# A graph layer on one core: which points of TensorE's order hold the gathers around the products with src rows

## The chip, the cores and the metric

The kernel runs on one core of one Trainium2 chip. The metric is the device time of one execution in microseconds (us), taken as the median of several runs; less is better.

## The reference

There are 12,500 nodes with 32 features and 400,000 directed edges, sorted by their target node. The layer normalizes the nodes' rows, passes each edge through a small network, and takes per node the maximum over its incoming edges:

```python
h = jnp.maximum(_layernorm(x), 0.0)
e_feat = jnp.concatenate([h[src], h[dst], edge_attr_32], axis=-1)   # 400000 x 96
hid = jax.nn.relu(e_feat @ W1 + b1)                                 # 96 -> 64
v = hid @ W2 + b2                                                   # 64 -> 32
x_cand = jax.ops.segment_max(v, dst, num_segments=12500)
return x + jnp.maximum(x_cand, h[:, -32:])
```

## The kernel before, in words

The edges are cut into four stripes that lie side by side on the 128 partitions (32 features each), and each stripe into 196 chunks of 512 edges. The main loop takes two chunks a turn, an even one and an odd one, so it has 96 full turns. The first layer is a sum of three products into the same four banks of accumulators (`ph`): the edges' own rows (`ea`, `edges_into`), the target rows (`of` against a small window `qf` of rows, `windows_into`), and the source rows (`ht`, `rows_into`). All three go through `into_ph`, line 837, with 8 matmuls each a turn, which the profile shows as 16 records.

The source rows `h[src]` are the costly part, and they are fetched in two ways. Of the 16 columns of 128 edges that a chunk has, 12 (in some chunks 11) are gathered by GpSimd with an indirect DMA each (line 186, `gh`). The other 4 or 5 are made on TensorE by products with one-hot matrices (`tile(c, m)`, line 351, 14 matmuls each), of which VectorE then picks the wanted row (a multiplication `one`, line 358, and a maximum, line 359). VectorE also transposes all rows into `ht` (lines 375 and 378).

A turn's order on TensorE is written out by hand (the scheduling is manual for all engines): products `ea`, `of`, `ht`; the transposes of finished results `tr` (line 703); the one-hot tiles `a1`, `a2`, `a3` of the even chunk; the second layer `l2` (line 871); two products `lv` (line 727); the tiles `b0` to `b3` of the odd chunk; and `n0`, the first tile of the next even chunk. GpSimd meanwhile issues the gathers for a later turn: 12 of the even chunk (slots 0 to 11) and 12 of the odd one (slots 12 to 23). Their buffers would let them run ahead, so a table, `HELD` (line 72), spreads them: it ties a slot to a point of another engine's order, and the gather in that slot waits until that point has been passed. `hold` looks a slot up, and `passes` records the instruction that is the point:

```python
def passes(iteration, name, ins):
    passed[iteration, name] = ins
def hold(c, i, ins):
    at = HELD.get(i + c % 2 * (K - MM))
    if at and c // 2 - at[0] >= 0:
        waiting.append((ins, (c // 2 - at[0], at[1])))
...
passes(c // 2, "ea", into_ph(ph, [(w1c, loaded[c + x][0]) for x in range(2)], True, False))
...
passes(c // 2, "ht", into_ph(ph, [(w1a, ht[x]) for x in range(2)], False, True))
```

In the table `b1` is the last matmul of that tile on TensorE, `b1 max` the last step on VectorE for it, `ea`, `ht`, `tr`, `lv` and `n0` are points on TensorE, `relu` is one on ScalarE and `scan` one on VectorE. The number ahead of the name says how many turns ahead of the gather's own turn the point lies (`n0` is recorded under a number one lower than its place would give, so 3 with `n0` is the end of the same turn as 3 with `b3`; the `ea` and `ht` with a 2 come right behind it). A slot without an entry waits for none of these points; it goes when the gather before it on GpSimd has been issued, its buffer is free and the gather eight before it has landed.

Of the kernel before, what the change touches and what calls it, by code (L numbers as in the profile page):

```python
# [68 lines left out]
END = LATE - 16  # L69
PIECE = 2 * A0  # L70
GP = 3
HELD = {0: (3, 'b1'), 1: (3, 'b1 max'), 2: (3, 'b2'), 3: (3, 'b2 max'), 4: (3, 'b3'), 5: (3, 'b3 max'), 6: (3, 'n0'),
        8: (2, 'ea'), 9: (2, 'ht'), 10: (2, 'tr'), 12: (2, 'relu'), 13: (2, 'a1'), 14: (2, 'a1 max'), 15: (2, 'a2'),
        16: (2, 'a2 max'), 17: (2, 'a3'), 19: (2, 'lv'), 20: (2, 'scan'), 21: (2, 'b0'), 22: (2, 'b0 max')}
BANKS = 7
SOON = {(3, 0): 'a0', (3, 6): 'a2', (4, 0): 'a3', (4, 6): 'b0', (5, 0): 'b1', (5, 6): 'b2'}
# [14 lines left out]
def gnn_kernel(ctx, tc, x, src, src_mm, src_x, src_t, dst, dst_end, dst_ext, lo, lo_c, ends_b, edge_attr, weights, w1, w2, b2, out):  # L91
# [133 lines left out]
# [4 lines that stand above are left out]
# [1060 lines left out]
```

## Time and profile before

| | |
|---|---|
| three timed runs | 3557.04, 3555.01, 3553.36 us |
| median | 3555.01 us |
| profiled execution | 3587.46 us, of which the span is 3585.7 us |
| instructions in the span | 55,025 |
| TensorE busy (matmuls; weight loads, which overlap them) | 3293.3 us (92%); 2511.2 us (70%) |
| VectorE, GpSimd, ScalarE busy | 2437.4 us (68%), 2161.2 us (60%), 1402.3 us (39%) |
| gathers, line 186 | 2249 instructions, 2123.6 us, 944 ns each |

The profiled execution took 32 us (0.9%) more than the median, so times within the trace are read against its own 3587.46. A line of the timeline gives the start, the time, the engine, the line, the operation and what it writes and reads; in brackets stands the idle time of the engine ahead of it and what seems to have ended it. "issue" means that the profile names nothing.

### The profile page before, as it was taken

The numbers are of one execution on the slowest core, as the hardware profiler recorded it, in microseconds if no ns is written. First come the engines' busy times: TensorE is split into PE (matmuls) and PEld (weight loads), VectorE is DVE, ScalarE is ACT, GpSimd is POOL, SyncE is SP. The second block draws the span as 40 slices with busy tenths as digits, with TensorE's granted clock in tenths as the row PEclk, the third lists the DMA queues.
The fourth block names the chain that finished last, engine by engine and source line by source line (L and its number), as shares of the span: only waits on it lengthen the run. The fifth ranks groups of instructions, "written<-read, shape, count | busy, mean of one in ns | idle before, by whom it ended". The sixth has DMA issues, their size and how long they took to land.

```text
span 3585.7 us, 55025 instructions
## 1 busy us (share of the span) xinstructions
PE 3293.3 (92%) x18468; PEld 2511.2 (70%) x18468; DVE 2437.4 (68%) x4987; ACT 1402.3 (39%) x2276; POOL 2161.2 (60%) x2295
## 2 busy tenths in 40 slices
PE   5788999999999999999999999999999999999996
PEld 3466767776767677767776767777767777677773
DVE  6467667767677677676666666767666766666765
ACT  4233434343443333434333334333333344343342
POOL 6665666665666666656666666666666666666562
PEclk8799999999999999999999999999999999999997
DMA  5322222222222222222222222222222222221222
GB/s 188 82 60 58 58 59 58 71 50 58 68 63 52 58 65 63 52 58 62 62 56 64 62 59 56 59 63 66 50 63 63 62 53 62 61 66 50 59 58 64
DMA packets 183894, 227.88 MB, mean 64 GB/s; under 512 B 115365, under 2 KB 155445, under 8 KB 170806
## 3 DMA queue, kind: packets, MB, share of 16 engines
q10 hardware_dynamic: 36228, 109.11, 9.6%
q0 software_dynamic: 72992, 37.52, 7.7%
q1 hardware_dynamic: 74386, 77.71, 7.0%
q8 instruction: 145, 2.38, 0.3%
q14 instruction: 143, 1.17, 0.1%
HBM read 212.63 MB, written 11.47 MB: 63 GB/s over the span
## 4 chain that ended last, share of the span: by engine, by line
PE 70%; DVE 12%; issue 8%; another core or an unknown queue 4%; DMA 1%; ACT 1%; POOL 1%; SPq 1%; DVEq 0%; ACTq 0%; POOLq 0%
PE pv L351 53%; PE ph L837 12%; DVE one L358 3%; PE pv L871 3%; DVE hot L311 2%; DVE pv L878 2%; DVE ht L375 1%; PE pv L727 1%; POOL gh L186 1%; DVE sm L885 1%; PE pv L703 1%; DMA top_d<-wo 1%; DVE gm L359 1%; DVE m L892 0%
## 5 line engine op out<-in xcount | busy, mean ns | idle before, releaser
L186 POOL DMA_INDIRECT gh<-h_d,src_i x2249 | 2123.6, 944 | 1355.9 <-issue 511.8
L351 PE MATMUL pv<-hs,hot 128*128 128x448 f32 x10752 | 2369.3, 378 | 112.5 <-issue 76.7
L351 PEld LDWEIGHTS pv<-hs,hot 128*128 128x128 f32 x10752 | 2096.1, 197 | 326.8 <-issue 127.0
L358 DVE TENSOR_TENSOR one<-pv,mask 128x448 f32<-128x448 f32 x768 | 470.4, 612 | 982.7 <-issue 340.1
L862 ACT ACTIVATE hid<-ph,wt 128x512 f32<-128x512 f32 x392 | 244.2, 687 | 982.0 <-remote 491.2
L359 DVE TENSOR_REDUCE gm<-one 128x32 f32<-128x448 f32 x768 | 476.3, 620 | 26.4
L311 DVE TENSOR_TENSOR hot<-kb,consts 128x1024 fp32r<-128x1024 f16 (+1 forms) x379 | 445.4, 1194 | 0.0
L837 PE MATMUL ph<-ht,wt 32*64 32x512 f32 x1568 | 350.4, 696 | 95.0 <-issue 59.3
L325 ACT ACTIVATE hot<-away,ones 128x512 fp32r<-128x512 f32 x582 | 421.8, 725 | 36.9 <-remote 17.9
L324 ACT ACTIVATE away<-kb,key_n 128x512 f32<-128x512 f16 x582 | 415.7, 714 | 0.0
L718 ACT ACTIVATE wo<-pv 128x256 f32<-128x256 f32 x95 | 36.5, 384 | 689.7 <-remote 383.9
L837 PEld LDWEIGHTS ph<-ht,wt 32*64 32x64 f32 x1568 | 84.1, 141 | 294.3 <-issue 246.2
L878 DVE TENSOR_TENSOR_SCAN pv<-pb,kept,pv 128x512 f32<-128x512 bf16 x193 | 244.0, 1264 | 15.1 <-remote 15.0
L375 DVE STREAM_TRANSPOSE ht<-gh 128x96 f32<-128x96 f32 x774 | 207.9, 269 | 2.6
L697 ACT ACTIVATE sb<-m,wt 128x128 f32<-128x128 f32 x97 | 39.1, 403 | 423.1 <-DVE sm L885 239.4
L351 PE MATMUL pv<-hs,xg 128*128 128x448 f32 x760 | 169.2, 366 | 8.1 <-issue 8.1
L351 PEld LDWEIGHTS pv<-hs,xg 128*128 128x128 f32 x760 | 143.1, 189 | 21.4 <-issue 11.6
L837 PE MATMUL ph<-of,qf 32*64 32x512 f32 x1552 | 136.3, 606 | 14.3 <-ACT of L672 11.2
L672 ACT ACTIVATE of<-of,ones 128x512 f32<-128x512 f32 x194 | 140.6, 725 | 6.3
L892 DVE TENSOR_REDUCE m<-sm 128x64 f32<-128x512 f32 x194 | 133.1, 686 | 6.7
L671 ACT ACTIVATE of<-db,below 128x512 f32<-128x512 int32 x194 | 137.4, 708 | 0.0
L837 PE MATMUL ph<-ea,wt 32*64 32x512 f32 x1568 | 131.3, 619 | 3.7 <-issue 2.6
(139 smaller groups left out, 1309.4 us busy)
## 6 DMA issues: line engine op xcount, KB each, us to landing
ea<-in_edge_attr SPq DMA_DIRECT2D x49, 1024.0 KB
db<-in_dst_ext ACTq DMA_DIRECT2D x48, 1024.0 KB
gh<-h_d,src_i POOLq DMA_INDIRECT x2249
pb<-pen_d ACTq DMA_DIRECT2D x47, 512.5 KB
kb<-key_d ACTq DMA_DIRECT2D x47, 512.0 KB
top_d<-wo SPq DMA_DIRECT2D x752, 3.0 KB
qf<-q_d SPq DMA_DIRECT2D x392, 16.0 KB
q_d<-qs SPq DMA_DIRECT2D x6, 512.0 KB
```

The lines of the kernel that those rows point to most:

```text
L186: ins = nc.gpsimd.indirect_dma_start(out=parts[-1][:, i, :], out_offset=None, in_=h_d[:, :], in_offset=bass.IndirectOffsetOnAxis(ap=src_i[ ...
L311: nc.vector.tensor_tensor(hot_of(c)[:, start:stop], keys[c][:, None, :].to_broadcast([P, n, MM * P]), key_ps[:, start:stop, None].to_broad ...
L324: nc.scalar.activation(away, keys[c], AF.Square, bias=key_n[:, k:k + 1])
L325: nc.scalar.activation(hot_of(c)[:, k], away, AF.Relu, bias=ones, scale=-1.0)
L351: ins = nc.tensor.matmul(po, hot[k], hs[:, part, k].rearrange("p f a -> p (f a)"), start=(k == 0 and part == 0), stop=(k == A1 - 1 and par ...
L358: nc.vector.tensor_tensor(one, of_group, mask[:, None, :].to_broadcast([P, D, A0]), op=ALU.mult)
L359: passes(c // 2 - 1, "ab"[c % 2] + str(m) + " max", nc.vector.tensor_reduce(row, one, axis=AX.X, op=ALU.max))
L375: nc.vector.transpose(ht[:, r].rearrange("p k e -> p (k e)"), gh[c][part][:, :r.stop - r.start].rearrange("p k f -> p (k f)"))
L672: nc.scalar.activation(of, of, AF.Relu, bias=ones, scale=-1.0)
L837: ins = nc.tensor.matmul(ph[s][x * HID:(x + 1) * HID], w[g], e[g], start=start, stop=stop)
L862: passes(c // 2, "relu", nc.scalar.activation(hid[k], of, AF.Relu, bias=b1c))
L878: ins = nc.vector.tensor_tensor_scan(pv, pen[:, :C], pv, -LOW if before is None else before, op0=ALU.add, op1=ALU.max)
```

## The change

Only the table changes. Slot 6 loses its hold (`n0`). Slot 8 is held by the products with src rows (`ht`) where it was held by those with edge rows (`ea`). Slot 9 loses its hold (`ht`). Slot 7 had none and has none. Slot 10 still waits for `tr`.

```diff
-HELD = {0: (3, 'b1'), 1: (3, 'b1 max'), 2: (3, 'b2'), 3: (3, 'b2 max'), 4: (3, 'b3'), 5: (3, 'b3 max'), 6: (3, 'n0'),
-        8: (2, 'ea'), 9: (2, 'ht'), 10: (2, 'tr'), 12: (2, 'relu'), 13: (2, 'a1'), 14: (2, 'a1 max'), 15: (2, 'a2'),
+HELD = {0: (3, 'b1'), 1: (3, 'b1 max'), 2: (3, 'b2'), 3: (3, 'b2 max'), 4: (3, 'b3'), 5: (3, 'b3 max'),
+        8: (2, 'ht'), 10: (2, 'tr'), 12: (2, 'relu'), 13: (2, 'a1'), 14: (2, 'a1 max'), 15: (2, 'a2'),
         16: (2, 'a2 max'), 17: (2, 'a3'), 19: (2, 'lv'), 20: (2, 'scan'), 21: (2, 'b0'), 22: (2, 'b0 max')}
```

On GpSimd, in the middle of the program, these are the slots 4 to 11 of chunk 112, whose holds lie around the products with src rows of one turn of the main loop. `DMASW` is the landing of an earlier gather, `PE` and `DVE` are the points of TensorE's and VectorE's order:

```order
 L186 DMA gh<-h_d,src_i 128x32 [waits DMASW1_49,PE_49]
 L186 DMA gh<-h_d,src_i 128x32 [waits DMASW2_49,DVE_49]
-L186 DMA gh<-h_d,src_i 128x32 [waits DMASW3_49,PE_49]
-L186 DMA gh<-h_d,src_i 128x32 [waits DMASW4_49]
-L186 DMA gh<-h_d,src_i 128x32 [waits DMASW5_49,PE_49]
-L186 DMA gh<-h_d,src_i 128x32 [waits DMASW6_49,PE_49]
+L186 DMA gh<-h_d,src_i 128x32 [waits DMASW3_49]
+L186 DMA gh<-h_d,src_i 128x32 [waits DMASW4_49]
+L186 DMA gh<-h_d,src_i 128x32 [waits DMASW5_49,PE_49]
+L186 DMA gh<-h_d,src_i 128x32 [waits DMASW6_49]
 L186 DMA gh<-h_d,src_i 128x32 [waits DMASW7_49,PE_49]
 L186 DMA gh<-h_d,src_i 128x32 [waits DMASW0_49]
```

No gather has moved in the row; slots 6 and 9 have lost their wait for TensorE, and slot 8's wait, which reads alike, is now for a later matmul.

On TensorE, the products and the transpose of that same turn stand as they stood. These are the rows of before, and those of the changed kernel are the same:

```order
L837 MATMUL ph<-ea,wt 64x512 [waits PE_49]
L837 MATMUL ph<-ea,wt 64x512
L837 MATMUL ph<-ea,wt 64x512 [waits DVE_49]
L837 MATMUL ph<-ea,wt 64x512
L837 MATMUL ph<-of,qf 64x512 [waits DMAHW4_49,Activation_49]
L837 MATMUL ph<-of,qf 64x512 [waits Activation_49]
...
L837 MATMUL ph<-ht,wt 64x512 [waits DVE_49]
L837 MATMUL ph<-ht,wt 64x512 x6
L703 MATMUL pv<-ident,sb 128x128 [waits PE_49]
```

Slot 8 was tied to the last row with `ea` here and is now tied to the last with `ht`, the row ahead of the transpose; the order of the matmuls has not moved.

## The prediction

> **What bounds the kernel now.** I read the page first: the engines' busy time, the chain of work that ended last, then the groups of the lines that the change touches.
>
> ```profile
> PE 3293.3 (92%) x18468; PEld 2511.2 (70%) x18468; DVE 2437.4 (68%) x4987; ACT 1402.3 (39%) x2276; POOL 2161.2 (60%) x2295
> ...
> PE 70%; DVE 12%; issue 8%; another core or an unknown queue 4%; DMA 1%; ACT 1%; POOL 1%; SPq 1%; DVEq 0%; ACTq 0%; POOLq 0%
> PE pv L351 53%; PE ph L837 12%; DVE one L358 3%; PE pv L871 3%; DVE hot L311 2%; DVE pv L878 2%; DVE ht L375 1%; PE pv L727 1%; POOL gh L186 1%; DVE sm L885 1%; PE pv L703 1%; DMA top_d<-wo 1%; DVE gm L359 1%; DVE m L892 0%
> ...
> L837 PE MATMUL ph<-ht,wt 32*64 32x512 f32 x1568 | 350.4, 696 | 95.0 <-issue 59.3
> L837 PE MATMUL ph<-of,qf 32*64 32x512 f32 x1552 | 136.3, 606 | 14.3 <-ACT of L672 11.2
> L837 PE MATMUL ph<-ea,wt 32*64 32x512 f32 x1568 | 131.3, 619 | 3.7 <-issue 2.6
> ```
>
> TensorE sets the time, with 70% of the chain. The gathers that the change moves (GpSimd, L186) carry 1% of it. What is odd is the products of L837: the three kinds (edge rows, `of` against `qf`, src rows) have nearly the same count and shape, yet those with src rows (`ht`) cost 350.4 us and 95.0 of idle before them, the others 131.3 with 3.7 and 136.3 with 14.3.
>
> The waits show who makes whom wait there (total us, count, longest):
>
> ```profile
> PEld ph L837 <- issue: 353.7, 692, 2.7
> ...
> POOL gh L186 <- PE ph L837: 114.0, 83, 4.0
> ```
>
> TensorE's weight loads of L837 wait 353.7 us for "issue", that is for nothing the profile names; the gathers wait 114.0 us for L837, and those are the waits the change redistributes.
>
> In the timeline I took three turns of the main loop: A, where the products begin at 1997.57, B at 2034.31 and C at 1712.78. In A:
>
> ```profile
> 1999.71 0.94 POOL L186 DMA_INDIRECT gh<-h_d,src_i  x1 [0.30 <-issue]
> ...
> 2000.96 0.94 POOL L186 DMA_INDIRECT gh<-h_d,src_i  x1 [0.31 <-issue]
> ...
> 2001.97 3.48 PE L837 MATMUL ph<-ht,wt 32*64 32x512 f32 x10 [0.82 <-issue]
> ...
> 2003.41 0.36 PEld L837 LDWEIGHTS ph<-ht,wt 32*64 32x64 f32 x8 [1.30 <-issue]
> 2003.74 0.94 POOL L186 DMA_INDIRECT gh<-h_d,src_i  x1 [1.84 <-PE ph L837]
> ...
> 2005.38 0.47 PE L703 MATMUL pv<-ident,sb 128*128 128x128 f32 x1
> ...
> 2005.74 0.94 POOL L186 DMA_INDIRECT gh<-h_d,src_i  x1 [1.06 <-PE ph L837]
> ```
>
> The gathers shown are slots 6, 7, 8 and 9. Slot 6 goes 0.30 us behind the one before, the pitch of an unbroken stream: its hold (`n0`) had long been met. TensorE has gaps of 0.82 and 1.30 us without a named cause while the stream runs, and goes on at 2003.41, 1.5 us after slot 7's gather ends (2000.96 + 0.94). In B the hold of slot 6 bites:
>
> ```profile
> 2034.32 0.94 POOL L186 DMA_INDIRECT gh<-h_d,src_i  x1 [0.30 <-issue]
> ...
> 2036.85 0.94 POOL L186 DMA_INDIRECT gh<-h_d,src_i  x1 [1.58 <-PE ph L837]
> ...
> 2038.03 0.33 PE L703 MATMUL pv<-ident,sb 128*128 128x128 f32 x1
> ...
> 2038.10 0.94 POOL L186 DMA_INDIRECT gh<-h_d,src_i  x1 [0.30 <-issue]
> 2039.34 0.94 POOL L186 DMA_INDIRECT gh<-h_d,src_i  x1 [0.30 <-issue]
> ```
>
> Slot 6 waits 1.58 us, slots 7 and 8 follow unbroken, and the products are through by 2038.03. The windows give what each costs (us, TensorE busy, weight loads busy, granted clock, DMA share, GB/s): first the products of L837 in A, B, C, then each turn's stretch from the `lv` products to its end.
>
> ```profile
> 1997.57:2005.38 7.81, 6.68 (x48) 1.74 (x48) 0.81 0.18 27
> 2034.31:2038.03 3.72, 3.57 (x48) 1.03 (x48) 1.00 0.41 69
> 1712.78:1718.45 5.67, 5.07 (x48) 1.55 (x48) 1.00 0.09 12
> ```
>
> ```profile
> 2017.41:2034.30 16.89, 16.89 (x86) 15.58 (x84) 14.88 (x29) 7.48 (x12) 10.12 (x11) 1.00 0.16 25
> 2048.42:2069.65 21.23, 19.12 (x86) 16.88 (x84) 15.98 (x33) 7.47 (x12) 12.78 (x14) 0.92 0.22 64
> 1728.48:1746.45 17.97, 17.45 (x86) 15.43 (x84) 15.22 (x28) 7.47 (x12) 10.44 (x12) 1.00 0.13 21
> ```
>
> B saves in the products and pays behind them: 21.23 us for the same 86 products that take 16.89 in A and 17.97 in C. That is the core of my argument: the hindrance goes with the stream of gathers, and where a pause ends it early, another stretch meets it later.
>
> **The change, part by part.** No instruction is added or removed; the rows of TensorE, VectorE, ScalarE and SyncE stay in order. Four holds on GpSimd change, and with 96 turns each is priced by the turns in which it bites.
>
> *Slot 6 without a hold.* The gathers of slot 6 that waited over 0.61 us number 26, the first and the last being
>
> ```profile
> 207.14 0.94 POOL L186 DMA_INDIRECT gh<-h_d,src_i  x1 [1.68 <-remote]
> ...
> 3434.48 0.95 POOL L186 DMA_INDIRECT gh<-h_d,src_i  x1 [1.43 <-PE pv L1058]
> ```
>
> In the other 70 turns the hold is inert, as in A, and its removal does nothing. In the 26 GpSimd saves some 1.4 us, worth nothing by itself since it is off the chain. The indirect effect is that the stream then runs through slots 6 and 7 into the products, as in A and C: B becomes an A or a C. Whole turns are A 2034.30 − 1997.57 = 36.73, B 2069.65 − 2034.31 = 35.34, C 1746.45 − 1712.78 = 33.67 us. So B to A costs 1.39 us and B to C gains 1.67; in 26 turns that is +36 to −43 us. I take the middle, (1.39 − 1.67) / 2 × 26 = −4 us, since nothing says which of the two a freed turn becomes. What bears the middle out are sums over seven turns (columns: us; busy TensorE, weight loads, VectorE, ScalarE, GpSimd; clock; DMA; GB/s), which hold 1, 3, 2 and 3 turns in which slot 6 waited:
>
> ```profile
> 1573.26:1824.81 251.55, 238.07 (x1345) 182.13 (x1338) 173.60 (x358) 99.46 (x161) 152.87 (x163) 0.95 0.24 60
> 1824.81:2075.45 250.64, 237.62 (x1344) 182.95 (x1337) 174.38 (x359) 98.95 (x161) 153.51 (x163) 0.94 0.24 62
> 2326.50:2575.86 249.36, 237.10 (x1345) 183.11 (x1339) 173.53 (x358) 98.96 (x161) 152.90 (x163) 0.95 0.24 60
> 3076.75:3329.31 252.56, 238.74 (x1344) 181.69 (x1338) 174.59 (x363) 99.21 (x161) 153.82 (x164) 0.95 0.24 60
> ```
>
> They lie between 249.36 and 252.56 with no trend: both ends have seven turns with two or three such waits.
>
> *Slot 8 behind `ht` instead of `ea`, slot 9 without a hold.* Where slot 8 waited for `ea` (A, C), it now waits until slot 9's old time, 2005.74 in A, and slot 9 goes one pitch later (0.94 + 0.30 = 1.24 us). In A that is 2.00 us for slot 8 and 1.24 for slot 9. Behind them slots 10 to 14 are also one pitch later. The stream has a pause that takes it up: slot 15 waits 1.65 us for `a2`.
>
> ```profile
> 2014.58 0.94 POOL L186 DMA_INDIRECT gh<-h_d,src_i  x1 [1.65 <-PE pv L351]
> ```
>
> 1.65 − 1.24 leaves 0.41, so slot 15 goes when it went. Price 0; if that cover is gone, GpSimd, busy for 60% of the span, is 1.24 us late until the next pause. Rows gathered now are used a turn later, and a lag of a pitch reaches TensorE only if VectorE's transposes wait for them, which 1% of POOL in the chain bounds. What queues behind the waiting slot 8 is GpSimd's stream alone: slots 9 and 10, then the rest. SP and ACT issue no DMA behind it.
>
> *The stretch of products freed of slot 8's issue.* In A slot 8 starts at 2003.74, 1.64 us ahead of the transpose (L703, 2005.38); in C likewise:
>
> ```profile
> 1717.71 0.95 POOL L186 DMA_INDIRECT gh<-h_d,src_i  x1 [1.99 <-PE ph L837]
> ...
> 1718.45 0.33 PE L703 MATMUL pv<-ident,sb 128*128 128x128 f32 x1
> 1719.45 0.94 POOL L186 DMA_INDIRECT gh<-h_d,src_i  x1 [0.79 <-PE pv L703]
> ```
>
> There it is 0.74 us at full clock, and A's clock is 0.81 over the products, which alone could make up the difference. TensorE has already recovered when slot 8 goes, in both. So I give this 0, with a gain of up to 0.74 us in the some 50 turns of the 70 whose slot 8 waits so (in the rest VectorE is late and slot 5 waits instead), −37 us, as the lower end, and as the upper end +0: a gather fewer beside the products has no way to lengthen them.
>
> **The sum.** −4 + 0 + 0 = −4 us. The profiled execution has a span of 3585.7 us and took 3587.46; the median of the three timed runs, 3555.01, is 32 us less, so the trace shows a somewhat more hindered run than the usual. Carried over to the median: 3555 − 4, about 3551 us. Less than 0.2% (7 us) either way can't be told from no change in this kernel; the forecast is no change.
>
> [...] The row first: over the products the clock was 0.81 in A and 1.00 in B and C, and A is the turn with the longest gaps. [...]
>
> **The rivals.** *Faster.* The product stretch is now clear of gathers from slot 7 to its end in every turn, and what hindered B later (21.23) goes as well: freed turns become Cs (33.67), and half of the 0.74 us of slot 8 comes too. For: C exists with slot 6 unheld. Against: the whole-turn sums don't fall where slot 6 waits less. Time: 26 × 1.67 × 0.5 = 22, or with 50 × 0.37 = 18 about 40; I put it at 3555 − 30 = 3525 us, from −10 to −50.
>
> *Slower.* Slots 8 to 14 one pitch later close the pause of 1.65 us at slot 15, where it is shorter than 1.24, and the stream then runs unbroken into the second layer and the `b` tiles, as in B: 21.23 − 16.89 = 4.34 us in each such turn. It decides from two turns up (8.7 us). For: B's stream ran so, and paid. Against: A's pause is longer than the lag. If 1 in 10 of the 70 other turns loses its pause: 7 × 4.34 = +30, 3585 us. Freed turns that become As give the same sign: 26 × 1.39 = +36, 3591 us.
>
> *It doesn't do what it says.* With slot 6 inert in 70 turns, and `ht`'s signal arriving with `ea`'s in the others (B: slot 8 unbroken), the order on the chip hardly differs: 3555 us. It shares the forecast's case.
>
> **How the numbers follow.** No change, inert or balanced: 0.37. Faster, gathers out of the products: 0.36, more than slower because both its parts have a row and the lower end lies further from 0 with the products' term. Slower, the pause lost or As for Bs: 0.27. Range: the faster case down to −35 us (3520, a tenth left out below), the slower up to +28 us (3583, a tenth above). For the likeliest case alone: 3548 to 3562.
>
> **What would show it.** In the trace of after: slot 6 at a gap of 0.30 in nearly all turns; slot 8 behind the `ht` products and slot 9 at 0.30 behind slot 8; L837 `ht` near 350 us or up to 26 × 2 = 50 us more, given back from `lv` to the turn's end; seven turns still 249 to 253 us. Wrong would be: `ht` far below 350 us (the slot-8 term was mis-sized), or seven-turn sums that leave that band either way, slot 15 without a pause being the sign of the slower case.

## The result and the profile after

The changed kernel took 3662.35 us (median of 4 runs, 3653.06 to 3665.07) against 3554.19 us before: a ratio of 1.0303, 95% interval 1.0279 to 1.0327, or 108 us slower. That is outside the predicted range. On four other Trainium2 chips, which the later experiments met, before takes 2938 us, and on the one of them where the changed kernel ran, so does it; this is told below, and it is the larger surprise.

The page of the changed kernel shows where to look: the engines' busy times, the chain of work that ended last, and the groups of L186 and of the products with src rows.

```profile
PE 3371.0 (92%) x18468; PEld 2546.1 (70%) x18468; DVE 2433.4 (67%) x4987; ACT 1399.3 (38%) x2276; POOL 2161.2 (59%) x2295
...
PE 76%; DVE 11%; issue 8%; another core or an unknown queue 2%; DMA 1%; POOL 1%; ACT 0%; DVEq 0%; SPq 0%; ACTq 0%; POOLq 0%
...
L186 POOL DMA_INDIRECT gh<-h_d,src_i x2249 | 2124.1, 944 | 1424.3 <-issue 545.5
...
L837 PE MATMUL ph<-ht,wt 32*64 32x512 f32 x1568 | 390.8, 752 | 112.8 <-issue 67.0
```

GpSimd issues the same gathers at the same 944 ns and still carries 1% of the chain. The products with src rows rose from 350.4 to 390.8 us. The waits of the changed kernel (total, times, longest, us):

```profile
PEld ph L837 <- issue: 439.0, 782, 10.7
POOL gh L186 <- PE ph L837: 214.2, 55, 6.7
```

TensorE's nameless waits in L837 went from 353.7 to 439.0 us, as more turns are hindered. The gathers' waits for L837 went from 114.0 to 214.2 us, which is the new hold of slot 8. In the timeline, the turn that was B in the prediction now reads:

```profile
2069.24 0.94 POOL L186 DMA_INDIRECT gh<-h_d,src_i  x1 [0.30 <-issue]
...
2070.49 0.94 POOL L186 DMA_INDIRECT gh<-h_d,src_i  x1 [0.30 <-issue]
...
2071.73 0.94 POOL L186 DMA_INDIRECT gh<-h_d,src_i  x1 [0.30 <-issue]
...
2072.76 0.22 PEld L837 LDWEIGHTS ph<-ht,wt 32*64 32x64 f32 x3 [1.28 <-issue]
...
2072.98 0.94 POOL L186 DMA_INDIRECT gh<-h_d,src_i  x1 [0.30 <-issue]
2074.19 0.13 PEld L837 LDWEIGHTS ph<-ht,wt 32*64 32x64 f32 x1 [1.21 <-issue]
...
2075.59 0.23 PEld L837 LDWEIGHTS ph<-ht,wt 32*64 32x64 f32 x7 [1.27 <-issue]
...
2076.90 0.48 PE L703 MATMUL pv<-ident,sb 128*128 128x128 f32 x1
...
2077.24 0.94 POOL L186 DMA_INDIRECT gh<-h_d,src_i  x1 [3.32 <-PE ph L837]
```

The gathers are slots 4 to 8. Slots 6 (2071.73) and 7 (2072.98) follow unbroken where slot 6 had paused, the products' weights come in drops with 1.2 to 1.3 us between them, and slot 8 waits 3.32 us for the end of the products. The window over its products (us, TensorE, weight loads, clock, DMA share, GB/s) was 3.72 us in B and is now:

```profile
2069.23:2076.90 7.67, 5.92 (x48) 1.71 (x48) 0.96 0.46 82
```

To see whether this is paid back, I compared the same turns by number, from the first record of the `ea` products to the next turn's, for 86 turns (numbers 5 to 90). 24 of them had a pause at slot 6 before; 48 had neither that nor a late VectorE; in 14 VectorE was late. The numbers are means in us, worked out from the records of each trace. A half-clock window is here an unbroken stretch for which the trace gives TensorE's granted clock as half; these last 6.1 us on the mean before and 5.6 after.

| the same turns | before | changed | only slot 6 dropped | only slots 8, 9 changed |
|---|---|---|---|---|
| 24 that had paused: products | 4.59 | 8.16 | 7.92 | 6.63 |
| ... transpose to second layer | 8.86 | 9.94 | 9.92 | 9.60 |
| ... second layer to the end | 20.71 | 18.79 | 17.80 | 19.73 |
| ... whole turn | 34.16 | 36.90 | 35.64 | 35.95 |
| 48 others: whole turn | 36.55 | 36.50 | 35.87 | 36.47 |
| 14 with VectorE late | 36.48 | 36.45 | 35.91 | 36.49 |
| half-clock windows in the span | 72 | 97 | 83 | 86 |

Between these two traces the other turns stand as they stood. The 24 turns that had paused are 2.74 us longer each, 66 us, and the spans differ by 3651.3 − 3585.7 = 65.6. So the loss between the two traces lies in those turns whole: 3.57 us more in the products, 1.08 in the tiles behind them, 1.92 back later. The timed difference is 42 us larger than that of the spans, because the first profile of before was 32 us above its median and that of the changed kernel 9 below its own. No trace shows where these 42 us lie. The column "only slot 6 dropped" gives a hint: there the 48 other turns are 0.68 us shorter each than before's (35.87 against 36.55), 33 us in all. If before's slow profile lost its 32 us in such turns, then a usual run of before loses something there to the change as well, and the 66 us are only the part of the 108 that the traces locate.

### The profile page after: what moved, and what is told of

Its sections match the earlier page's. It is cut to its first block, busy times and chain, and to the rows that moved or that the text cites. A ratio compares the mean times of both kernels' runs of the same rounds, so it can differ in the third digit from the quotient of the medians.

```text
span 3651.3 us, 54835 instructions
## 1 busy us (share of the span) xinstructions
PE 3371.0 (92%) x18468; PEld 2546.1 (70%) x18468; DVE 2433.4 (67%) x4987; ACT 1399.3 (38%) x2276; POOL 2161.2 (59%) x2295
## 4 chain that ended last, share of the span: by engine, by line
PE 76%; DVE 11%; issue 8%; another core or an unknown queue 2%; DMA 1%; POOL 1%; ACT 0%; DVEq 0%; SPq 0%; ACTq 0%; POOLq 0%
PE pv L351 56%; PE ph L837 15%; PE pv L871 3%; DVE one L358 2%; DVE pv L878 2%; DVE hot L311 1%; PE pv L727 1%; PE pv L703 1%; DVE ht L375 1%; DVE sm L885 1%; DMA q_d<-qs 1%; DVE m L892 1%; POOL gh L186 1%; DVE gm L359 0%
## 5 line engine op out<-in xcount | busy, mean ns | idle before, releaser
L186 POOL DMA_INDIRECT gh<-h_d,src_i x2249 | 2124.1, 944 | 1424.3 <-issue 545.5
L351 PE MATMUL pv<-hs,hot 128*128 128x448 f32 x10752 | 2383.8, 380 | 80.0 <-issue 46.9
L351 PEld LDWEIGHTS pv<-hs,hot 128*128 128x128 f32 x10752 | 2120.3, 199 | 281.3 <-issue 80.0
L837 PE MATMUL ph<-ht,wt 32*64 32x512 f32 x1568 | 390.8, 752 | 112.8 <-issue 67.0
L837 PEld LDWEIGHTS ph<-ht,wt 32*64 32x64 f32 x1568 | 93.0, 150 | 333.6 <-issue 281.3
L837 PE MATMUL ph<-of,qf 32*64 32x512 f32 x1552 | 159.2, 638 | 21.7 <-issue 19.3
L351 PE MATMUL pv<-hs,xg 128*128 128x448 f32 x760 | 165.9, 363 | 1.4 <-issue 1.3
L351 PEld LDWEIGHTS pv<-hs,xg 128*128 128x128 f32 x760 | 142.6, 188 | 12.7 <-issue 3.0
L837 PE MATMUL ph<-ea,wt 32*64 32x512 f32 x1568 | 134.4, 626 | 9.4 <-issue 9.3
```

Source lines behind the costliest of these rows:

```text
L186: ins = nc.gpsimd.indirect_dma_start(out=parts[-1][:, i, :], out_offset=None, in_=h_d[:, :], in_offset=bass.IndirectOffsetOnAxis(ap=src_i[ ...
L351: ins = nc.tensor.matmul(po, hot[k], hs[:, part, k].rearrange("p f a -> p (f a)"), start=(k == 0 and part == 0), stop=(k == A1 - 1 and par ...
L837: ins = nc.tensor.matmul(ph[s][x * HID:(x + 1) * HID], w[g], e[g], start=start, stop=stop)
```

## The experiments

The diffs are against the kernel before, in the table `HELD`, unless the text names another. The first four ran on a chip where before takes 3555.22 us, as it did for the prediction; I call it the first chip.

**Only slot 6.**

```diff
-5: (3, 'b3 max'), 6: (3, 'n0'),
+5: (3, 'b3 max'),
```

> Only the hold of slot 6 is dropped; slots 8 (ea) and 9 (ht) stay held as before. Theory 'pause': the loss came from the 24 or so turns in which slot 6 waited and its pause let the products with src rows through (1.73 us there, 3.55 in the like turns after the change) and spared the turn a half-clock window; then this kernel has no pause at slot 6, some 97 half-clock windows against 72 before, and 3630 to 3665 us. Theory 'lag': the loss came from slots 8 to 14 going a pitch later; then this kernel stays within 15 us of before, 3540 to 3570 us.

Measured: 3576.05 us, ratio 1.0056 (1.0039 to 1.0072). Between the two theories: slower, but by 21 us. The profiled span, 3578.2 us, is 7 us below that of before's slow profile, so the traced numbers below compare turns and don't add up to the 21. The windows over the products and from `lv` to the end of the turn that was B:

```profile
2024.17:2031.64 7.47, 6.20 (x48) 1.75 (x48) 0.83 0.37 80
```

```profile
2043.63:2060.53 16.90, 16.90 (x87) 15.58 (x85) 14.95 (x32) 7.48 (x12) 10.18 (x11) 1.00 0.24 52
```

The products are as hindered as in the changed kernel (7.67), but the stretch behind falls from B's 21.23 to 16.90, the unhindered length. Here the gain is mostly given back, as I had forecast for the whole change: in the 24 turns 3.33 us more, 2.91 us less behind, and 1.06 in between at half clock.

**Only slots 8 and 9.**

```diff
-8: (2, 'ea'), 9: (2, 'ht'),
+8: (2, 'ht'),
```

> Slot 6 keeps its hold (n0); slot 8 waits for ht, slot 9 for nothing. Theory 'pause': about 24 turns keep the pause at slot 6, half-clock windows stay near 72, 3540 to 3575 us. Theory 'lag': the whole loss is here, 3630 to 3665 us. If both have a part, the excesses of this kernel and of the one that drops slot 6 alone add up to about 108 us.

Measured: 3617.22 us, ratio 1.0168 (1.0148 to 1.0187). Theory "lag" asked for 3630 us or more and isn't met. Theory "pause" alone, as I had put it, fails as well: 62 us come from the holds that I priced at nothing. But the trace shows that they act through the same pause. In the 24 turns slot 5 now starts 1.01 us behind the products' start, where it was 0.23 ahead. So `n0` has been met by the time slot 6 is reached, and 12 of the 24 pauses are gone; those turns take 2.49 us more, the 12 that kept it 1.09 more, and 46 of the 48 others 0.01. That is 12 x 2.49 + 12 x 1.09 = 43 us, and this profile's span, 3629.1, is 43 us above that of before. The lag that I had thought taken up at slot 15 reaches slot 5 of the next round: in the turn ahead of each of the 24, slots 9 to 12 go 0.79 us later than before on the mean, and slot 22 still 0.76. The rest of slot 5's 1.24 us is mostly that turn itself, which is 0.43 us shorter.

The two parts make 21 + 62 = 83 of the 108 us. Together they cost more: without the hold of slot 6 the late slots 8 and 9 lengthen the stretch behind the second layer in the 24 turns from 17.80 to 18.79, and the other 48 turns from 35.87 to 36.50.

**A pause at slot 6 in every turn.**

```diff
-6: (3, 'n0'), 8: (2, 'ea'), 9: (2, 'ht'),
+6: (2, 'ea'), 8: (2, 'ht'),
```

> The changed kernel with slot 6 held by the products with edge rows (ea) of the turn, a point right behind n0. Theory 'pause': the pause then comes in most turns, not in 24 only; products from their start to the transpose fall from 7.4 us to 4.6 to 6, half-clock windows from 97 to under 60, and the time to 3480 to 3560 us, part of it paid back behind the products (20.7 against 18.6 us there). Theory 'lag': slots 8 to 14 are as late as in the changed kernel, so 3640 us or more.

Measured: 3552.87 us, ratio 0.9998 (0.9986 to 1.0009). One hold at slot 6, put 16 records later in TensorE's order, takes back the whole 108 us of the changed kernel. (The number expected for theory "lag" isn't a test here, since the gathers are no longer late: slot 12 goes 11.45 us behind the start of the products on the mean, against 13.01 in the changed kernel and 11.73 before.) Slot 6 waits in all 72 turns without a late VectorE, products take 4.48 us on the mean (7.40 in the changed kernel, over the same 86 turns), and there are 55 half-clock windows (97). But the stretch from the second layer on takes 22.24 us (19.09), so that nothing is gained over before. Windows of two turns that follow each other, the products and the stretch from `b0` (us, TensorE, weight loads, VectorE, ScalarE, GpSimd, clock, DMA, GB/s):

```profile
2013.07:2018.12 5.05, 4.84 (x50) 1.48 (x50) 4.95 (x10) 0.07 (x1) 2.81 (x4) 1.00 0.47 76
2028.39:2052.04 23.65, 20.85 (x86) 17.23 (x84) 17.94 (x40) 7.46 (x12) 12.99 (x14) 0.86 0.20 58
```

```profile
2052.04:2055.18 3.14, 3.14 (x50) 1.09 (x50) 3.04 (x8) 0.00 (x0) 1.89 (x2) 1.00 0.24 36
2065.45:2085.41 19.96, 18.05 (x86) 15.42 (x84) 14.77 (x27) 7.48 (x12) 12.58 (x14) 1.00 0.11 16
```

The same 86 products take 23.65 us in the one and 19.96 in the other, against 16.90 unhindered, and the long one is at clock 0.86: this time the half-clock windows fall there.

**No gather beside the products.**

```diff
-6: (3, 'n0'), 8: (2, 'ea'), 9: (2, 'ht'),
+6: (2, 'ht'),
```

> Slots 6 to 9 all wait behind the products with src rows (6 is held by ht, 7 to 9 by nothing): no gather is issued beside them once slot 5 is out. Theory 'pause': products fall to 4 to 5 us in nearly all turns, half-clock windows under 40, 3450 to 3540 us, unless the stream, 2.5 us later at slot 12, loses its other pauses, which would bring it back to about 3560. Theory 'lag': slots 10 to 14 are 2.5 us later than in the changed kernel, and the time is above 3665 us.

Measured: 3656.97 us, ratio 1.0278 (1.0249 to 1.0308). My theory's number fails: the products are nearly free (4.04 us) but the stretch from the second layer takes 23.82 us, and there are 102 half-clock windows. Theory "lag" doesn't explain it: slot 12 goes 11.98 us behind the start of the products, 0.25 us later than before and 1.0 us earlier than in the changed kernel, where I had expected 2.5 us later, and still the kernel loses 102 us. The timeline shows what a long unbroken stream does, here beside the tile `b0`:

```profile
2078.80 0.95 POOL L186 DMA_INDIRECT gh<-h_d,src_i  x1 [3.57 <-PE pv L703]
...
2088.48 1.17 PE L351 MATMUL pv<-hs,hot 128*128 128x448 f32 x5
...
2088.80 0.95 POOL L186 DMA_INDIRECT gh<-h_d,src_i  x1 [0.30 <-issue]
...
2090.10 0.46 PE L351 MATMUL pv<-hs,hot 128*128 128x448 f32 x1 [0.45 <-issue]
...
2090.80 0.47 PE L351 MATMUL pv<-hs,hot 128*128 128x448 f32 x1 [0.24 <-issue]
2091.30 0.95 POOL L186 DMA_INDIRECT gh<-h_d,src_i  x1 [0.31 <-issue]
2091.50 0.36 PE L351 MATMUL pv<-hs,hot 128*128 128x448 f32 x1 [0.23 <-issue]
...
2092.90 0.36 PE L351 MATMUL pv<-hs,hot 128*128 128x448 f32 x1 [1.04 <-issue]
...
2094.32 3.95 PE L351 MATMUL pv<-hs,hot 128*128 128x448 f32 x11 [0.34 <-issue]
```

The stream starts at 2078.80 and is unbroken. For its first eight gathers the tiles run at full pace; from the tenth (2090.05) matmuls start 0.70 us or twice that apart, and they are free again at 2094.32, 2.07 us after the last gather ends (2091.30 + 0.95). Over the whole trace, counting pauses of over 0.41 us between the starts of two matmuls of L351 less the 0.20 that is usual, and leaving out the first gather of a run and what lies behind its last: 4 us lost in 1471 us beside the second to seventh gather of a run, 7 of 87 beside the eighth and ninth, 155 of 214 from the tenth on. Behind the last gather of the runs of ten and more, until the next gather, another 170 of 246 us are lost. The place in the turn isn't the reason: beside the one tile `b0`, in the six traces of this chip together, 14 of 602 us are lost beside the second to seventh gather of a run, 43 of 263 beside the eighth and ninth, 137 of 192 from the tenth on (186 of these 192 us lie in this kernel). Beside the products it begins earlier: in turn A of the prediction the gaps stand beside the sixth and seventh gather of a run. So on this chip the price of a gather goes with the length of the run ahead of it, and this ties the holds together: a pause moved away from one place makes the run longer at the next.

**A break in the long run, and the other holds: on a second chip.** Four more kernels of this kind, the kernel before among them, met another chip. The first is the changed kernel with one more edit, shown against the changed kernel:

```diff
-13: (2, 'a1'), 14: (2, 'a1 max'), 15: (2, 'a2'), 16: (2, 'a2 max'),
+13: (2, 'a2 max'),
```

> The changed kernel with slot 13 held by the maximum of a2 (a2 max) in place of a1, and slots 14 to 16 held by nothing: slots 8 to 16, which go nearly unbroken in the changed kernel, get a pause of 0.6 to 1.9 us in their middle. Theory 'runs' (TensorE loses its time late in a long unbroken run of gathers, eight and more beside the one-hot tiles): the stretch from the second layer to the turn's end falls from 19.1 us to about 18.5, and the time to 3590 to 3635 us. Theory 'lag' (what costs is that GpSimd is later): slots 13 to 16 are another 1 us later, and the time is 3660 us or more.

The next is before with `6: (2, 'ea')` for `6: (3, 'n0')`:

> The kernel before with slot 6 held by ea in place of n0; slot 8 (ea) and slot 9 (ht) as before. It differs from the third experiment (six_ea, 3553 us) only in slots 8 and 9. If moving slot 8 behind ht costs about 60 us on its own, as in the second experiment, this kernel takes 3480 to 3500 us. Theory 'runs', by which that cost comes from products already hindered and from the run behind them (nine gathers there, eight here): within 30 us of 3553, on the faster side, 3525 to 3553 us.

Then the third experiment with `13: (2, 'a3')` and nothing for 14 to 17:

> The third experiment (slot 6 behind ea, slot 8 behind ht) with slot 13 held by a3 and slots 14 to 17 by nothing, so that the run from slot 8 to 16 is broken by a pause of about 2 us where the one-hot tiles of the even chunk end. Theory 'runs': the stretch from the second layer to the turn's end falls from 22.2 to 20 or 21 us, and the time to 3450 to 3530 us. Theory 'lag': slots 13 to 16 are 2 us later, 3570 us or more.

And the kernel before, unchanged:

> The kernel before, unchanged, for a second profile, since the first took 3587 us where the timed runs have 3555. All theories: about 3555 us. Theory 'pause': 60 to 70 half-clock windows (72 in the first profile) and 24 to 35 turns in which slot 6 waits (24 there).

Measured: 2938.29, 2937.75, 2941.02 and 2938.29 us, where before's timed runs there gave 2938.23; ratios of 1.0003, 1.0003, 1.0006 and 0.9998, all with 1 inside the interval. No theory had this: before itself is 617 us faster than on the first chip. Its page there:

```profile
PE 2858.3 (97%) x18468; PEld 2369.3 (81%) x18468; DVE 2437.4 (83%) x4987; ACT 1396.8 (48%) x2276; POOL 2162.3 (74%) x2295
...
PE 91%; DMA 4%; DVE 2%; ACT 1%; issue 1%; POOL 0%; SPq 0%; ACTq 0%; DVEq 0%; POOLq 0%
...
L186 POOL DMA_INDIRECT gh<-h_d,src_i x2249 | 2124.9, 945 | 710.7 <-issue 384.5
```

GpSimd and VectorE are busy as long as on the first chip (2162.3 and 2437.4 us), a gather takes 945 ns as there, and "issue" fell from 8% of the chain to 1%. A turn's products in the timeline:

```profile
1649.96 0.94 POOL L186 DMA_INDIRECT gh<-h_d,src_i  x1 [0.30 <-issue]
1650.29 0.23 PEld L837 LDWEIGHTS ph<-ea,wt 32*64 32x64 f32 x16 [0.30 <-issue]
...
1651.21 0.94 POOL L186 DMA_INDIRECT gh<-h_d,src_i  x1 [0.30 <-DVE one L358]
...
1652.06 0.18 PEld L837 LDWEIGHTS ph<-ht,wt 32*64 32x64 f32 x8 [0.25 <-issue]
1652.46 0.94 POOL L186 DMA_INDIRECT gh<-h_d,src_i  x1 [0.30 <-issue]
1653.05 0.33 PE L703 MATMUL pv<-ident,sb 128*128 128x128 f32 x1
```

The gathers go unbroken across the products, and these take 1653.05 − 1650.29 = 2.76 us. 1986 us of the tiles' time lie beside the tenth or a later gather of a run, and 0.3 us of it are lost. The stream hinders nothing on this chip. GpSimd goes nearly without a pause there: a turn takes 29.47 us on the mean, and its 23 or 24 gathers at 1.25 us take 28.8 to 30.0. So the holds hardly bite: in the 86 turns slot 6 waited over 0.61 us 9 times.

**The changed kernel again, with two others: on a third chip.**

> The changed kernel once more, since kernels that differ only in the holds all took 2938 us on a second chip, where before took 2938 as well and the sequencers' register moves, up to 0.72 us on the first chip, took 0.03 us. Theory 'hindered sequencers': the loss of 108 us needs that hindrance; where before takes 2938 us this kernel takes 2933 to 2944 us, and where before takes 3555 it takes 3645 to 3670. Rival: the later gathers cost something of their own, and this kernel is slower by 10 us or more on either chip.

> The changed kernel with slot 13 held by a2 max and slots 14 to 16 by nothing, again. Where before takes 2938 us: the same as before. Where before takes 3555 us: theory 'runs' 3590 to 3635 us, the stretch from the second layer to the turn's end at 18.5 us against 19.1; theory 'lag' 3660 us or more.

> The kernel before with slot 6 held by ea in place of n0, again. Where before takes 2938 us: the same as before. Where before takes 3555 us: 3480 to 3500 us if moving slot 8 behind ht costs about 60 us on its own; 3525 to 3553 us by theory 'runs'.

Measured: 2938.31, 2938.83 and 2937.09 us with before at 2938.79. The changed kernel's ratio is 0.9995 (0.9985 to 1.0004). As theory "hindered sequencers" has it, nothing is lost where the stream hinders nothing. The rival isn't tested by it, though: with GpSimd's stream nearly unbroken, slot 8 waited over 0.61 us in 11 of 86 turns, so hardly any gather goes later for the change on this chip. TensorE's waits for "issue" in L837 in this run of the changed kernel:

```profile
PEld ph L837 <- issue: 126.2, 480, 0.8
```

126.2 us with none above 0.8, against 439.0 and 10.7 on the first chip.

**No holds at all, and the others once more: on a fourth and a fifth chip.**

```diff
-HELD = {0: (3, 'b1'), ...
+HELD = {}
```

> The table HELD is empty: no gather waits for a point of another engine's order. Where before takes 2938 us (a chip whose sequencers aren't hindered): the same, 2930 to 2945 us, since the gathers go unbroken there with the table too. Where before takes 3555 us: by theory 'runs' there are then no pauses but those of full buffers, and the time is 3700 us or more; by theory 'lag' (lateness of the gathers costs) nothing is late, and the time is 3555 us or less.

> The changed kernel with slot 13 held by a2 max and slots 14 to 16 by nothing. Where before takes 2938 us: the same as before. Where before takes 3555 us: theory 'runs' 3590 to 3635 us; theory 'lag' 3660 us or more.

> The empty table HELD again, for a chip where before takes 3555 us: theory 'runs' 3700 us or more; theory 'lag' 3555 us or less. Where before takes 2938 us: the same as before.

> The kernel before with slot 6 held by ea, for a chip where before takes 3555 us: 3480 to 3500 us if moving slot 8 behind ht costs about 60 us on its own; 3525 to 3553 us by theory 'runs'. Where before takes 2938 us: the same as before.

Measured: 2938.67, 2938.83, 2937.72 and 2938.79 us with before at 2938.16 and 2938.31. Without any hold the ratio is 0.9999 (0.9989 to 1.0009). The table does nothing there; on the second and third chips, where it was read from the traces, its holds hardly bite (slot 6 in 9 of 86 turns, slot 8 in 11). The kernel without holds, the one before with slot 6 held by `ea` and the broken runs never met the first chip, so they could not test "runs" against "lag" there. Nor did any run come back to the first chip at a later time, so what differs may lie in the chip or in its state at that hour.

## Why the prediction was wrong, point by point

*What bounds the kernel.* Right: TensorE, hindered beside the stream of gathers, and a pause at slot 6 lets the products through. The trace after and the first four experiments bear it out. What I didn't see is that this belongs to the chip of the profile (or its state then) and not to the kernel alone.

*Slot 6 without a hold.* Two terms of the sum failed, and this is the first: "I take the middle, (1.39 − 1.67) / 2 × 26 = −4 us, since nothing says which of the two a freed turn becomes". Dropped alone, the hold cost 21 us in the timed runs; with the whole change the freed turns became 2.74 us longer each, more than either end. I had made the two ends from single turns, C among them, the third quickest of the 48 other turns. The means of the same trace pointed the way: 34.16 us for a turn that pauses and 36.55 for the 48 others, 2.39 more. Dropping the hold alone cost 1.48 us in each of the 24 turns (35.64 − 34.16), near A's 1.39, though against before's slow profile. (The waits of slot 6 number 28 and not 26: two lie outside the first and last shown, at 171.17 and 3470.84. This changes the term by less than 1 us.)

*The seven-turn sums* were the wrong witness. One pause more or less moves a sum by some 2.4 us (36.55 − 34.16), and the sums spread over 3.2 us for other reasons, so that four of them could show no trend.

*The clock.* The sum has no term for it, though the prediction's windows had 0.81 over A's products. There are 97 half-clock windows after and 72 before, 25 more, for 24 pauses gone. What sets such a window off, no run shows. Matmuls of the tiles (L351) start 0.37 us apart inside them and 0.20 outside, at the median of both traces, so I take half of the windows' length as the most that they can cost, an estimate: it went from 220.9 to 269.7 us, or 49 us. In the 24 turns it went from 0.56 to 2.77 us each. Of these 2.21 us more, 1.21 lie in the tiles behind the products, which are 1.08 us longer: there the slow clock can account for the whole loss, 26 us in all. Another 1.07 lie within the products, where TensorE also waits, so that their cost isn't shown. Turn C, which kept its clock with a gap of 1.36 us ahead of its weight loads where A's longest is 1.30, was an exception: 44 of the 48 other turns before had a stretch at half clock.

*Slots 8 and 9.* The second term that failed, and the larger: "Price 0" was wrong by 62 us when tried alone. I followed the lag to the pause of slot 15 and stopped there; 0.76 us of it still stood at slot 22, it went on to slot 5 and helped to take away half of the pauses at slot 6. The rival "slower" had the right sign and cause (late slots close a pause further on) but another pause, and half the size (+30). The sum also took the parts as independent; together they cost 25 us more than each alone.

*"a gather fewer beside the products has no way to lengthen them"* didn't hold over the whole trace: with slots 8 and 9 moved, products with src rows rose from 350.4 to 376.2 us alone, and from 367.9 to 390.8 where slot 6 has no hold. It held in the 48 other turns when tried alone: their products fell from 7.74 to 7.28 us, within the 0.74 that the prediction allowed, but the stretch from the second layer rose from 18.39 to 18.98, and the turn stayed as it was.

*Still open.* What in the first chip, or in its state then, lets a stream of gathers hinder TensorE; why before's first profile was 32 us above its median, and with it where 42 of the 108 us lie; and how the 25 us that the two parts cost only together divide into longer runs and later gathers. A pause in the run from slot 8 on was to tell that, and it has run only where nothing is hindered.

## What to carry to other kernels

Where pauses in one engine's stream depend on who comes first, a change of a wait must be followed around the whole loop to the next turn's waits, and the price of a pause be read from the same turns by number, with their clock, not from neighbours. Before tuning the order around a wait that the profile can't name ("issue"), run the kernel on a second chip: here none of the tables tried made a difference on four chips of five, the empty one on the two where it ran. Beside a stretch that slows TensorE, count the half-clock windows that follow it: here the tiles behind the products lost 1.08 us a turn by them.

## What the hardware showed that I had not expected

- One program, one instruction stream: 3555 us on one chip, 2938 us on four others, at equal times per gather (944 and 945 ns) and equal busy time of VectorE (2437.4 us on the first and the second chip).
- On the slow chip SyncE's register moves lag too while gathers are issued: of 1232 the slowest tenth take 0.43 us or more and the slowest hundredth 0.71 (the slowest of all 1.15), where on the second chip 0.03 us holds for both. None of the 63 that lie more than 2.2 us behind a gather's end took over 0.03 us. 0.70 us is also the spacing of the hindered matmuls.
- On that chip TensorE's hindrance comes late in a run of gathers (from the eighth to the tenth beside the tile `b0`, at the sixth in turn A's products), outlasts the last one by 1.5 and 2.1 us in the two places shown, and then half clock often follows: in 23 of the 24 turns after the change, in 8 of them before.
- On the second chip a run has no such price: in before's profile there 0.3 of 1986 us are lost beside the tenth and later gathers.
